# Four 512x512 weight products per group rewritten in Strassen's seven-product scheme in a cross-attention and RWKV kernel

## The chip, the cores and the metric

The kernel runs on one core of a Trainium2 chip. The metric is the device time of one execution in microseconds (us), and less is better. Arithmetic is in float32 throughout. The engines are PE (TensorE, matrix products), DVE (VectorE), ACT (ScalarE), POOL (GpSimd) and SP (SyncE, which here only issues transfers).

## The reference

There are 32 sequences of 128 tokens with 512 features. A first layer normalizes each sequence and its context, and forms an attention with a 512x512 score matrix per sequence. A second layer is an RWKV block over them:

```python
xa = _ln(x, ln1_w, ln1_b)
sx = concat([state[:, 1:2] - xa[:, :1], xa[:, :-1] - xa[:, 1:]])
xxx = tanh((xa + sx * maa_x) @ maa_w1)          # five low-rank mixes
xk, xw, xv, xr, xg = xa + sx * (maa_stack + xxx @ maa_w2)
w = exp(-exp(time_decay + tanh(xw @ td_w1) @ td_w2))
r, k, v = xr @ Wr.T, xk @ Wk.T, xv @ Wv.T
g = silu(xg @ Wg.T)                             # gates
out = recurrence over time of (r, k, v, w, u)
x1 = x + groupnorm(out) * g @ Wo.T
xc = _ln(x1, ln2_w, ln2_b)                      # feed-forward part
xk2, xr2 = xc + sx2 * ffn_maa_k, xc + sx2 * ffn_maa_r
rr = sigmoid(xr2 @ Wfr.T)
kk = square(relu(xk2 @ Wfk.T))
return x1 + rr * (kk @ Wfv.T)
```

All of `Wr, Wk, Wv, Wg, Wo, Wfk, Wfr, Wfv` are 512x512. The change concerns the products with `Wg`, `Wfk`, `Wfr` and `Wfv`.

## The kernel before, in words

The 32 sequences go through in 8 groups of four (`G = 4`), so that a group has N = 512 tokens. `layer0(b)` is the first layer for one sequence, and `layer1(g, xs)` the RWKV block for one group. In the block, activations lie with 128 features on the partitions and the 512 tokens of the group along the row: an activation is four such tiles (`NC = 4`). The sequences of the next group are worked off inside the current one (`ahead`), so that PE has independent work at any moment. The feed-forward part (`feed_forward`) of a group has three stages, `norm`, `squares` (`Wfk`) and `rows` (`Wfr`, `Wfv`). That of the last group but one is held back (`later`) and used as filler inside the last group, which has no next group.

A product with a whole weight is 16 matmuls of 128x128 against 512 columns. `proj` takes the weight's blocks as the held side and streams the tokens; its output has features on the partitions. The stages `head` and `rows` hold the token blocks and stream the weight, so that their output has tokens on the partitions, as the output array wants it. Four matmuls accumulate in one bank of PSUM, which has eight banks of 128x512 (`banks`). In the stage `gates`, ACT takes the sigmoid of each bank and DVE multiplies it with the bank. In `squares`, ACT takes relu of the bank and DVE multiplies it with the bank once more. In `rows`, ACT takes the sigmoid of the `Wfr` bank, DVE multiplies it with the `Wfv` bank, POOL adds the residual, and SP issues the transfer out.

The `mixes` stage between front and gates puts five mixed inputs into four tiles each: DVE reads a bank and one tile, POOL adds `xa`. That is 20 additions of 128x512 per group on POOL.

Weights are read from HBM into a ring of four 1 MB tiles (`weights`, `W_SLOTS`), once per group. Working tiles of 128x512 come from a pool of 44 (`work`, `T_SLOTS`), tiles of twice the width from a pool of 3 (`wides`).

Nothing is issued when it is written. `Program.record` (line 246, which is why nearly every row of the profile has that line) collects every operation, and `schedule` puts them in order with an own table of durations (`cost`), the delays between engines (`LAGS`), the slots of the pools, and shifts of each stage's rank (`SHIFTS`). The result is one fixed order per engine, in which each engine then waits for what it needs. `pace` makes some transfers wait for a PE instruction.

Of the kernel before, what the change touches and what calls it, by code (L numbers as in the profile page):

```python
# [12 lines left out]
F32 = mybir.dt.float32  # L13
# [16 lines left out]
DM, NMIX, DD = 32, 5, 64  # L30
C = 64
LEVELS = (4, 8, 16, 32)
T_SLOTS, SMALL_SLOTS, W_SLOTS, WIDE_SLOTS = 44, 40, 4, 3
# [30 lines left out]
    "first0": -306, "first0+": -95, "first1": 2, "first1+": -122, "first2": -40,  # L64
    "first2+": -7, "first3": 24, "first3+": 203, "front": 7, "front+": 157, "gates": -67,
    "gates+": -1, "head": -121, "head+": 51, "levels0": -68, "levels0+": -71, "levels2": 20,
    "levels2+": -152, "mixes": 81, "mixes+": -41, "norm": 78, "norm+": -310,
    "outputs0": -277, "outputs0+": 238, "outputs2": -235, "outputs2+": -661,
    "recurrence0": -14, "recurrence0+": -48, "recurrence2+": -68, "rows": 85, "rows+": 306,
    "squares": -88, "squares+": 77, "values0": -56, "values0+": -63, "values2": 33,  # L70
    "values2+": 81,
# [82 lines left out]
class Fixed(Pool):  # L154


    def shaped(self, slot, shape):
        return self.tiles[0]
# [450 lines left out]
def xattn_then_rwkv(ctx: ExitStack, tc: tile.TileContext, a: dict, out: bass.AP):  # L609
# [9 lines left out]
    work = Pool(slots("t", T_SLOTS, [P, 512]))  # L619
    small = Pool(slots("small", SMALL_SLOTS, [P, 64]))  # L620
    rks = Pool(slots("rk", 2, [P, 4 * N]))
    wides = Pool(slots("wide", WIDE_SLOTS, [P, 2 * N]))
    weights = Pool(slots("wring", W_SLOTS, [P, NC * E]))
# [16 lines left out]
    def st_(*shape):  # L640
        return View(Tensor(small, [P, *shape]))
# [9 lines left out]
    for n in ("WnT", "WmT", "Wl0", "WoT0"):  # L651
        w0[n] = const.tile([P, P], F32, tag=n, name=n)
        nc.scalar.dma_start(w0[n], a[n])
# [26 lines left out]
    wv = fixed("wv", [P, NC, E])  # L680

# [92 lines left out]
    def weight(n, after):  # L774
        K.held = after
        t = View(Tensor(weights, [P, NC, E]))
        K.sync.dma_start(t, a[n + "T"].rearrange("(c p) o -> p c o", p=P))
        return t
# [98 lines left out]
    def proj(w, xm, eo):  # L877

        pp = bank()
        for ci in range(NC):  # L880
            K.tensor.matmul(
                pp, w[:, ci, eo * P : (eo + 1) * P], xm[ci], start=(ci == 0), stop=(ci == NC - 1)
            )
        return pp

# [16 lines left out]
    def recurrence(c, ex, xk, xr, xv, wk, wr, s0m):  # L902
# [5 lines left out]
        for i in range(2):  # L908
            K.scalar.copy(r[i], proj(wr, xr, c + i))
            K.scalar.copy(k[i], proj(wk, xk, c + i))  # L910
            K.scalar.copy(v[i], proj(wv, xv, c + i))
# [189 lines left out]
    def layer1(g, xs):  # L1101
# [41 lines left out]
        wg, wk, wr = (weight(n, begun[g * G + 1]) for n in ("Wg", "Wk", "Wr"))  # L1143
# [77 lines left out]
        gates = []  # L1221
        for c in range(NC):
            pg = proj(wg, xm["g"], c)
            gate = wt()
            K.scalar.activation(gate, pg, AF.Sigmoid)
            K.vector.tensor_tensor(gate, pg, gate, ALU.mult)
            gates.append(gate)

        o = []
        for c in range(0, NC, 2):  # L1230
            K.stage = ("recurrence", g, str(c))
            if g == NG - 1 and c == 2:
                last_ws[:] = [weight(n, holds) for n in ("Wfk", "Wfr")]
            holds = K.ops[-1]
# [11 lines left out]
        if g == NG - 1:  # L1246
            last_ws.append(weight("Wfv", third))
        elif g < NG - 2:
            ws = [weight(n, third) for n in ("Wfk", "Wfr", "Wfv")]

# [28 lines left out]
        for i in range(G):  # L1279
            px1 = bank()  # L1280
            for c in range(NC):
                K.tensor.matmul(
                    px1, o[c][:, i * L : (i + 1) * L], wo[:, c, :],
# [7 lines left out]
        if g == NG - 2:  # L1291
            later.append(feed_forward(g, xs, last_ws))
        else:
            place(3)
            for _ in feed_forward(g, xs, ws if g < NG - 1 else last_ws):
                pass
        return following

    later, last_ws = [], []

    def feed_forward(g, xs, ws):

        K.stage = ("norm", g, "")
# [13 lines left out]
        kk = []  # L1317
        for eo in range(NC):
            pk = proj(ws[0], xk2, eo)
            t = wt()  # L1320
            K.scalar.activation(t, pk, AF.Relu)
# [71 lines left out]
```

## Time and profile before

| what | value |
|---|---|
| median of 3 runs | 1794.67 us (1794.45 to 1796.84) |
| profiled execution | 1798.06 us, of which its span is 1796.3 us |
| granted PE clock in it | 0.995 |
| PE busy | 1758.5 us, 98% of the span |
| DVE, ACT, POOL busy | 1171.4, 706.2 and 310.3 us |
| moved by DMA | 87.23 MB, mean 49 GB/s |

The span runs from the first to the last instruction of the profiled execution. A float32 matmul shows up as two PE records, each with its own load of the held side (engine PEld): 512 matmuls are x1024. In a row's names the streamed operand comes first and the held one second: `bank<-t,wring` streams an activation past weights, `bank<-wring,t` streams a weight past activations. Records of PE overlap each other in the trace, so that the mean of one record is longer than the distance from one to the next.

### The profile page before, as it was taken

The numbers are of one execution on the slowest core, as the hardware profiler recorded it, in microseconds if no ns is written. First come the engines' busy times: TensorE is split into PE (matmuls) and PEld (weight loads), VectorE is DVE, ScalarE is ACT, GpSimd is POOL, SyncE is SP. The second block draws the span as 40 slices with busy tenths as digits, with TensorE's granted clock in tenths as the row PEclk, the third lists the DMA queues.
The fourth block names the chain that finished last, engine by engine and source line by source line (L and its number), as shares of the span: only waits on it lengthen the run. The fifth ranks groups of instructions, "written<-read, shape, count | busy, mean of one in ns | idle before, by whom it ended". The sixth has DMA issues, their size and how long they took to land. (4 is left out here: it accounts for less than half of the span.)

```text
span 1796.3 us, 45435 instructions
## 1 busy us (share of the span) xinstructions
PE 1758.5 (98%) x20232; PEld 888.7 (49%) x20232; DVE 1171.4 (65%) x2301; ACT 706.2 (39%) x1230; POOL 310.3 (17%) x329
## 2 busy tenths in 40 slices
PE   8999999999999999999999999999999999899998
PEld 4435554456434554345543465445554345445543
DVE  9847784468935687456864578546784765786561
ACT  4524531356313563235632445324542245324321
POOL 2230014200150001600006000160010500320011
PEclk9999999999999999999999999999999999899999
DMA  6000131012120130101211022110221201001010
GB/s 206 21 0 3 37 119 62 9 41 73 59 70 1 41 108 26 69 2 53 96 47 47 2 58 90 53 41 2 63 85 59 73 25 49 3 0 61 15 36 35
DMA packets 61940, 87.23 MB, mean 49 GB/s; under 512 B 20336, under 2 KB 21488, under 8 KB 61744
## 3 DMA queue, kind: packets, MB, share of 16 engines
q1 hardware_dynamic: 61024, 84.06, 14.7%
q8 instruction: 158, 2.59, 0.6%
q14 instruction: 38, 0.31, 0.1%
q10 hardware_dynamic: 720, 0.26, 0.1%
HBM read 75.93 MB, written 8.39 MB: 47 GB/s over the span
## 5 line engine op out<-in xcount | busy, mean ns | idle before, releaser
L246 PE MATMUL bank<-t,wring 128*128 128x512 f32 x1024 | 469.0, 603 | 2.0 <-DVE t L246 2.0
L246 PE MATMUL bank<-wring,t 128*128 128x512 f32 x768 | 339.6, 595 | 0.7 <-DVE t L246 0.7
L246 PEld LDWEIGHTS bank<-t,wring 128*128 128x128 f32 x1024 | 187.2, 190 | 239.1 <-issue 205.4
L246 POOL TENSOR_TENSOR t<-t,t 128x512 f32<-128x512 f32 x192 | 239.4, 1285 | 349.3 <-DVE t L246 343.3
L246 DVE TENSOR_TENSOR t<-bank,t 128x512 f32<-128x512 f32 (+1 forms) x256 | 143.7, 585 | 211.4 <-PE bank L246 164.1
L246 POOL TENSOR_TENSOR small<-small,neg_half 128x1 f32<-128x1 f32 (+1 forms) x96 | 62.9, 661 | 1131.4 <-DVE small L246 1131.3
L246 PE MATMUL bank<-t,t 128*128 128x512 f32 x512 | 251.1, 607 | 2.1 <-ACT t L246 1.9
L246 PEld LDWEIGHTS bank<-wring,t 128*128 128x128 f32 x768 | 143.5, 190 | 185.7 <-issue 179.1
L246 ACT COPY t<-bank 128x512 f32<-128x512 f32 (+1 forms) x240 | 132.2, 589 | 218.3 <-PE bank L246 212.1
L246 ACT ACTIVATE t<-bank 128x512 f32<-128x512 f32 x120 | 71.4, 598 | 341.4 <-PE bank L246 341.3
L246 DVE SCALAR_TENSOR_TENSOR t<-bank,vec,t 128x512 f32<-128x512 f32 x192 | 131.4, 743 | 67.2 <-PE bank L246 67.2
L246 PEld LDWEIGHTS bank<-ident,t 128*128 128x128 f32 x900 | 104.5, 141 | 75.2 <-issue 43.6
L246 PE MATMUL bank<-ident,t 128*128 128x128 f32 x900 | 130.1, 276 | 4.6 <-ACT t L246 2.7
L246 ACT ACTIVATE wide<-rk,par 128x512 f32<-128x512 f32 x128 | 85.4, 715 | 122.4 <-DVE rk L246 122.4
L246 ACT ACTIVATE t<-bank,small 128x512 f32<-128x512 f32 x128 | 87.8, 690 | 106.2 <-DVE small L246 105.4
L246 PEld LDWEIGHTS bank<-t,t 128*128 128x128 f32 x512 | 87.0, 189 | 85.6 <-issue 56.3
L246 PEld LDWEIGHTS bank<-wide,rk 32*64 32x64 f32 x8192 | 95.6, 131 | 55.3 <-ACT wide L246 17.0
L246 PE MATMUL bank<-t,wv 128*128 128x512 f32 x256 | 122.6, 603 | 0.0
L246 DVE COPY_PREDICATED at<-level,bank 128x512 f32<-128x512 int32 x192 | 121.5, 704 | 0.0
L246 PE MATMUL bank<-wide,rk 32*64 32x64 f32 x8192 | 105.9, 233 | 8.2 <-issue 3.8
L246 DVE TENSOR_REDUCE small<-bank 128x1 f32<-128x512 f32 x128 | 85.9, 680 | 30.8 <-PE bank L246 30.4
L246 DVE SCALAR_TENSOR_TENSOR t<-t,vec,t 128x512 f32<-128x512 f32 x128 | 90.9, 755 | 0.1
(98 smaller groups left out, 1796.4 us busy)
## 6 DMA issues: line engine op xcount, KB each, us to landing
t<-in_ctx_dram SPq DMA_DIRECT2D x32, 256.0 KB, 3.2
t<-in_x_dram SPq DMA_DIRECT2D x32, 256.0 KB, 3.0
wring<-in_WgT_dram SPq DMA_DIRECT2D x8, 1024.0 KB, 5.2
wring<-in_WkT_dram SPq DMA_DIRECT2D x8, 1024.0 KB, 5.3
wring<-in_WrT_dram SPq DMA_DIRECT2D x8, 1024.0 KB, 5.2
wring<-in_WoT_dram SPq DMA_DIRECT2D x8, 1024.0 KB, 5.6
out_dram<-t SPq DMA_DIRECT2D x32, 256.0 KB, 2.0
wring<-in_WfkT_dram SPq DMA_DIRECT2D x7, 1024.0 KB, 5.2
```

Source lines behind the costliest of these rows:

```text
L246: done[op] = f(*[real(x) for x in args], **{k: real(x) for k, x in kw.items()})
```

## The change

The four products are computed with seven products of half the size in each direction instead of eight, in the form with 15 additions (Winograd's form of Strassen's scheme). Both sides are cut into four quarters of 256x256. One product of quarters is four matmuls of 128x128 against 256 columns, so that a weight takes 28 matmuls of 256 columns, where it took 16 of 512.

The seven combinations of the weight's quarters are computed once, in the first group, by four additions on POOL, and the ones that are no quarter are saved in HBM (`saved`). Later groups read all seven, 256 KB each (`seven`). The combinations of the activations (`s1`, `s2`, `s4` and one in place) are formed on POOL, as eight additions of 128x256 per product. The sums of the products are formed partly in PSUM, by going on accumulating in a bank after ACT has copied it out (`p1`, `p5`, `u2`, `u3`), partly by DVE from a bank and a copy, and one of them on POOL.

The other stages follow from that. The gates are now multiplied on POOL from tiles, after a sigmoid of a tile. The squares are two ACT passes over double-width tiles. The rows come out as four tiles of two sequences and half the features: DVE multiplies, POOL adds the residual in two halves, and SP writes 256 KB. The ring of weights becomes 16 tiles of 256 KB, `Wk`, `Wr` and `Wo` being read in four pieces, and the wide pool has 6 tiles. The transfers of the feed-forward weights are ordered after the operation `after` in front of its `norm` stage; before, they were ordered after one in the recurrence (`third`). The planner's shifts are other numbers.

```diff
+H = 256
+LEFT, RIGHT = ("Wg", "Wfk"), ("Wfr", "Wfv")
-T_SLOTS, SMALL_SLOTS, W_SLOTS, WIDE_SLOTS = 44, 40, 4, 3
+T_SLOTS, TINY_SLOTS, SMALL_SLOTS, W_SLOTS, WIDE_SLOTS = 43, 36, 6, 16, 6
...
-    weights = Pool(slots("wring", W_SLOTS, [P, NC * E]))
+    weights = Pool(slots("wring", W_SLOTS, [P, 2 * H]))
...
+    def seven(n, g, after):
...
+        left = n in LEFT
+        if g:
+            return [
+                piece(saved[n, i] if (n, i) in saved else quarter(*QUARTERS[left][i]))
+                for i in range(7)
+            ]
+        q11, q12, q21, q22 = (piece(quarter(i, j)) for i in range(2) for j in range(2))
+        s1, s2, s4 = (View(Tensor(weights, [P, 2, H])) for _ in range(3))
+        if left:
+            K.gpsimd.tensor_tensor(s1, q12, q22, ALU.add)
+            K.gpsimd.tensor_tensor(s2, s1, q11, ALU.subtract)
+            K.gpsimd.tensor_tensor(s4, q21, s2, ALU.subtract)
+            K.gpsimd.tensor_tensor(q12, q11, q12, ALU.subtract)
+            got = [q11, q21, s1, s2, s4, q12, q22]
...
+    def winograd(w, x, to, left=True):
+        def part(i, j):
+            return [x[2 * i + k][:, j * H : (j + 1) * H] for k in range(2)]
+        s1, s2, s4 = (wt([P, 2, H]) for _ in range(3))
...
+        if left:
+            steps = [(s1, x12, x11, ALU.subtract), (s2, x22, s1, ALU.subtract)]
+            steps += [(x12, x22, x12, ALU.subtract), (s4, x21, s2, ALU.subtract)]
+            sides = [x11, x21, s1, s2, x22, x12, s4]
...
+        for to_, one, other, op in steps:
+            for k in range(2):
+                K.gpsimd.tensor_tensor(to_[k], one[k], other[k], op)
+        def product(i, into, first):
+            with K.bunch(1720):
+                for m in range(2):
+                    for k in range(2):
+                        of_m = slice(m * P, (m + 1) * P)
+                        one, other = (
+                            (w[i][:, k, of_m], sides[i][k]) if left
+                            else (sides[i][k][:, of_m], w[i][:, k])
+                        )
+                        K.tensor.matmul(
+                            into[:, m], one, other, start=first and m == 0 and k == 0,
+                            stop=k == 1, skip_group_check=True,
+                        )
...
+        pb = new_bank()
+        product(0, pb, True)
+        p1 = copy(pb)
+        pa = new_bank()
+        product(1, pa, True)
+        K.vector.tensor_tensor(to(0, 0), pa, p1, ALU.add)
+        pc = new_bank()
+        product(2, pc, True)
+        p5 = copy(pc)
+        product(3, pb, False)
+        u2 = copy(pb)
+        product(4, pc, False)
+        K.vector.tensor_tensor(to(0, 1), pc, u2, ALU.add)
+        product(5, pb, False)
+        u3 = copy(pb)
+        K.gpsimd.tensor_tensor(to(1, 1), u3, p5, ALU.add)
+        pd = new_bank()
+        product(6, pd, True)
+        K.vector.tensor_tensor(to(1, 0), pd, u3, ALU.add)
...
-            pg = proj(wg, xm["g"], c)
-            gate = wt()
-            K.scalar.activation(gate, pg, AF.Sigmoid)
-            K.vector.tensor_tensor(gate, pg, gate, ALU.mult)
+        winograd(
+            seven("Wg", g, begun[g * G + 3]), xm["g"],
+            lambda i, j: gates[i].view(j * H, (N, 2), (1, H)),
+        )
+        for gate in gates:
+            t = wt()
+            K.scalar.activation(t, gate, AF.Sigmoid)
+            K.gpsimd.tensor_tensor(gate, gate, t, ALU.mult)
...
-            pk = proj(ws[0], xk2, eo)
-            t = wt()
-            K.scalar.activation(t, pk, AF.Relu)
-            K.vector.tensor_tensor(t, t, pk, ALU.mult)
+        winograd(seven("Wfk", g, after), xk2, lambda i, j: kk[i].view(j * H, (N, 2), (1, H)))
+        for t in kk:
+            for func in (AF.Relu, AF.Square):
+                K.scalar.activation(t, t, func)
...
+        winograd(seven("Wfr", g, after), xr2, lambda i, j: rr[i][j], left=False)
+        for t in rr[0] + rr[1]:
+            K.scalar.activation(t, t, AF.Sigmoid)
+        winograd(seven("Wfv", g, after), kk, lambda i, j: y[i][j], left=False)
+        for i in range(2):
+            for j in range(2):
+                t, first = y[i][j], g * G + 2 * i
+                K.vector.tensor_tensor(t, t, rr[i][j], ALU.mult)
+                for m in range(2):
+                    K.gpsimd.tensor_tensor(
+                        t[:, m], t[:, m], xs[2 * i + m][:, j * H : (j + 1) * H], ALU.add
+                    )
```

## The prediction

> **What bounds the kernel now.** I read the page's first section, then the list of PE's own waits, then the windows of one group, and only then single rows.
>
> ```profile
> PE 1758.5 (98%) x20232; PEld 888.7 (49%) x20232; DVE 1171.4 (65%) x2301; ACT 706.2 (39%) x1230; POOL 310.3 (17%) x329
> ...
> PE bank L246 <- issue: 8.2, 11, 1.4
> PE bank L246 <- DVE t L246: 8.2, 7, 2.0
> PE bank L661 <- DMA WoT<-in_WoT_dram: 6.1, 1, 6.1
> PE bank L246 <- ACT t L246: 4.7, 10, 1.8
> ```
>
> PE is busy for 98% of the span, and its waits add up to some 30 us, of which 6.1 are the first transfer. The chain that ended last says little here: for its last 180 us it is PE alone. So the order that the planner made keeps PE filled, and the time is PE's streaming time. What PE no longer streams is gained, unless something else becomes late.
>
> ```profile
> 725.00:762.00 37.00, 36.95 (x117) 14.09 (x117) 17.55 (x26) 8.46 (x11) 29.66 (x24) 1.00 0.16 57
> ...
> 1538.00:1640.00 102.00, 94.08 (x1329) 46.02 (x1330) 81.51 (x135) 34.70 (x53) 27.94 (x25) 0.95 0.01 2
> ```
>
> The columns after the window are length, PE, PEld, DVE, ACT, POOL, clock, DMA share, GB/s. The first window is one group's mixes: POOL is busy for 29.66 of 37 us, although its mean is 17%. The second is the last group's front, mixes and first recurrence, where less filler is left: there PE loses 8 us, and DVE is at 80%. Those are the two tight places.
>
> **PE's part: what is removed and added.**
>
> ```profile
> 499.64 10.89 PE L246 MATMUL bank<-wring,t 128*128 128x512 f32 x25
> 899.68 6.17 PE L246 MATMUL bank<-wring,t 128*128 128x512 f32 x14
> 1293.25 1.73 PE L246 MATMUL bank<-wol,t 128*128 128x128 f32 x14
> 862.61 0.39 PE L246 MATMUL bank<-wol,t 128*128 128x128 f32 x2
> ```
>
> From start and length of uninterrupted runs: 512 columns take (10.89 - 6.17) / 11 = 0.429 us per record, 128 columns (1.73 - 0.39) / 12 = 0.112 us. No 256-column float32 record exists. Between the two rows a straight line gives 0.2175; half of 512 gives 0.2145. I take 0.2165.
> Removed: 4 products x 8 groups x 16 matmuls x 2 records = 1024 x 0.429 = 439.4 us. Added: 4 x 8 x 28 x 2 = 1792 x 0.2165 = 388.0 us. Saved: 51 us (49.6 with 0.2175, 55 with 0.2145).
>
> A rule of the Trainium skill speaks against this step. "TensorE: Matmul & The Clock Gate", sections "LDWEIGHTS" and "Back-to-back issue gap": a load takes about columns / 1.2 ns, so 107 ns for 128, and the spacing of load and matmul pairs is set by both. In series 0.2165 would become 0.32 us, the added part 578 us and the kernel 139 us slower. The row decides: the 128-column run has a new held side for each record, and still has 0.112 us per record. So a load shorter than the stream behind it is hidden there, and 256 columns leave twice the cover. PEld rows of this kind have 190 ns, still under 216.
>
> **The other engines, per group.**
> - POOL gains 32 additions of 128x256, 4 sums `u3 + p5`, 4 gate multiplications; the residual additions only change shape. Whole ones have 1285 ns. A half has no row: it lies between 0.6 (a one-column operation, 597 ns) and 1.27, and I take 0.68, a little over half. That is 32 x 0.68 + 8 x 1.27 = 32 us, 256 us in all, and 16 x 1.27 = 20 us for the weights of the first group. POOL goes from 310 to about 585 us, 33%.
> - DVE loses 12 multiplications with a bank and gains 12 sums from a bank and 4 multiplications of tiles (0.69 each): +2.8 us, 22 us in all, 68%.
> - ACT gains 16 copies (589 ns) and 1.8 us in the squares (4 passes of 1057 ns for 4 of 598): +11 us, 90 us in all, 45%.
> - DMA: each product reads 1.75 MB where it read 1 MB, about 24 MB more on 87; the engines' share goes from some 15% to 19%. Next group's `Wk` and `Wr` hold 8 of the 16 ring slots during a feed-forward, so that its 21 pieces turn over in the other 8: one slot every 14 us, while a 256 KB transfer lands in 3.0 to 3.2 us. SP issues some 460 transfers in place of 175; behind one that waits for its slot stand the next pieces, `Wo` and the outputs, with some 10 us to spare each. I cost this at nothing; if the cover were gone, each late piece would cost PE up to 3 us.
> None of these sums binds, each lying beside PE. What counts is what is late locally.
>
> **What POOL and DVE do to each other.**
>
> ```profile
> L246 DVE SCALAR_TENSOR_TENSOR t<-bank,vec,t 128x512 f32<-128x512 f32 x192 | 131.4, 743 | 67.2 <-PE bank L246 67.2
> L246 DVE TENSOR_TENSOR t<-rk 128x512 f32<-128x512 f32 x48 | 31.7, 686 | 5.2 <-PE bank L246 4.3
> L246 DVE TENSOR_TENSOR t<-wide 128x512 f32<-128x512 f32 x16 | 15.5, 971 | 55.4 <-ACT wide L246 55.4
> ...
> 757.66 3.75 POOL L246 TENSOR_TENSOR t<-t,t 128x512 f32<-128x512 f32 x3
> 760.37 1.59 DVE L246 TENSOR_TENSOR t<-wide 128x512 f32<-128x512 f32 x1 [5.79 <-ACT wide L246]
> ```
>
> The second and third rows are the same work, both operands from SBUF, and yet 686 and 971 ns. The `t<-wide` one sometimes comes when POOL is still at the mixes: the one at 760.37 takes 1.59 us and ends 0.55 us after POOL's last, so it waited for POOL. The mixes' own operation, with one operand from PSUM, runs beside POOL throughout at 743. "SBUF — State Buffer", section "SBUF: two separate sides", has the rule: a DVE operation with two SBUF inputs and a GpSimd one take one port pair in turn, and the loser is blocked for the other's whole instruction. That speaks against putting the additions on POOL.
> By the rule: in one feed-forward POOL has 24 x 0.68 + 3 x 1.27 + 8 x 0.68 = 25.6 us, and DVE about 25 operations of the blocked kinds (12 mixes at 0.75, 3 shifts, 4 multiplications at 0.69, some scalings), 17 us. In turn 43 us, beside 3 x 28 x 2 x 0.2165 = 36.4 us of PE plus some 3.4 us of the next group's scores. Read strictly, 3 us are lost per group. By the trace, a hit costs about 0.9 us (1.59 - 0.69), and what it does to PE depends on who is next. So I go through it. In the new order the eight additions for `Wfk` stand beside eight DVE mixes of `xk2`, `xr2` and the next front. In turn they take 8 x (0.68 + 0.75) = 11.4 us, not 5.4. Then s1 comes 1.4 us late and s2 by 0.5 us; DVE comes some 5.5 us late to the sum that frees the bank which the seventh `Wfk` product reuses, and PE waits about 1.9 us for it. After that PE has 12 us of `Wfr` products, which cover relu, square and the additions for `Wfv`. So 0 to 2.4 us are lost per group, and I take 1.7: 14 us in all. The mixes give little: their DVE operations read PSUM, and PE has some 36 us of work beside POOL's 31 from the first mix to the last gate product. The gate multiplications fall on the start of the recurrence: 4 us in all. The first group has 15 us more on POOL in its feed-forward (12 weight additions): 4 us. The last group and the tail (one more DVE step of 0.7 us between the last product and the transfer): 2 us.
>
> **Sum.** 1796.3 - 51 + 24 = 1769 of span, -27 us. The profiled run had 1798.06 us, 3.4 above the median of the runs, so I apply the difference to the median: 1794.7 - 27 = 1767.7, rounded to 1767.
>
> **The rivals.**
> A, the forecast (0.50): 8 to 38 of the 51 us come back as short PE waits, most in the feed-forward stages. 1752 to 1782.
> B (0.32): nearly all is kept, because PE's fillers cover the lateness, as they do now in the crowded mixes window (36.95 of 37 us). At most 8 us come back, and up to 55 are saved: 1740 to 1752. For it: the waits of before are only 30 us in 1796. Against it: those fillers were as long, and the additions on POOL were not there.
> C, the slower side (0.18, of which 0.08 slower): the port in turn. Its place is the stretch from the first `Wfk` addition to the last gate product, where POOL now has some 63 us (25.6, then 20 mixes at 1.27 and 12 for the gates) beside about 92 of PE (48.5 for the four products, the rest scores, mixes and the first projections of the recurrence). It decides from 51 / 8 = 6.4 us per group; at 8 us per group the time is 1795 + 13 = 1808. For it: the strict sum of 43 us against 40. Against it: DVE's sums read a bank, and that kind was never slowed.
> That the change doesn't do what it says can be left aside: the new order has 896 matmuls of 256 columns and 512 fewer of 512.
>
> The measurement of this kernel can tell about 0.2% (3.6 us). Faster by more: A, B and a third of C, 0.88. Within: 0.04. Slower: 0.08. The range leaves out the upper half of C and a sliver of B: 1742 to 1789.
>
> **What would show it.** Right: PE rows of 128x256 whose runs have 0.215 to 0.218 us per record; PE busy near 1710 us; POOL near 585; PE's waits grown to 50 or 60 us, most of them on POOL and DVE tiles around the `Wfk` products; the DVE rows with two tile operands with a longer mean than 755 ns. Wrong: a 256-column pitch over 0.23; PE waits on DMA of `wring`; PE's waits as small as before (B), or over 80 us (C).

## The result, and the profile after

The changed kernel takes 1820.77 us (median of three runs, 1813.12 to 1821.34) against 1794.67: a ratio of 1.0129, 95% interval 1.0086 to 1.0171. It is some 26 us slower; the prediction had it 27 us faster.

The page of the changed kernel, busy time by engine. The helper that records every operation, L246 before, is L252 here.

```profile
PE 1730.7 (95%) x21000; PEld 1039.4 (57%) x21000; DVE 1275.9 (70%) x2333; ACT 797.2 (44%) x1363; POOL 643.6 (35%) x697
```

PE's own waits (us in total, times, longest):

```profile
PE bank L252 <- POOL t L252: 23.9, 11, 5.7
PE bank L252 <- ACT t L252: 16.2, 16, 4.7
PE bank L252 <- DVE t L252: 13.8, 22, 1.3
PE bank L252 <- issue: 10.1, 13, 2.7
PE bank L672 <- DMA t<-in_WoT_dram: 6.1, 1, 6.1
PE bank L252 <- DMA wring<-Wfv: 4.1, 4, 1.2
```

These and four small ones add up to 78 us where they were 32, and they come from four sides at once. No engine is full: POOL, whose new additions will turn out to be the largest part of the cause, is idle for 65% of the span. The 11 waits on POOL are only 24 of the 78 us.

Two windows, one around a steady group's feed-forward additions and one at the last group (columns: length, PE, PEld, DVE, ACT, POOL, granted clock, DMA share, GB/s). The first row is the kernel before, at the same time of its run; the other two are the changed kernel. The last window has the bounds of the one that the prediction called tight.

```profile
695.00:711.00 16.00, 16.00 (x50) 7.03 (x49) 13.67 (x28) 5.27 (x9) 0.54 (x1) 1.00 0.01 2
695.00:711.00 16.00, 12.49 (x58) 10.37 (x57) 15.97 (x23) 5.29 (x9) 13.55 (x14) 1.00 0.32 93
1538.00:1640.00 102.00, 96.18 (x985) 49.95 (x983) 63.43 (x113) 32.30 (x52) 39.33 (x39) 0.95 0.03 9
```

In the last window PE is busy for 96.18 us where it was 94.08, so this stretch did not get worse. In the steady group DVE is busy for 15.97 of 16 us and POOL for 13.55, while PE has 3.5 us without work. This is how a shared resource looks in a table by engine: both sharers seem busy, because an instruction that waits inside itself counts as busy. The single rows show it. From the trace of the changed kernel, start, length, engine, operation, count, and in brackets the idle time before the first of them and what ended it:

```profile
694.84 8.80 PE L252 MATMUL bank<-t,wring 128*128 128x256 f32 x40
694.28 6.88 DVE L252 SCALAR_TENSOR_TENSOR t<-t,vec,t 128x512 f32<-128x512 f32 x6
694.90 10.91 POOL L252 TENSOR_TENSOR t<-t,t 128x256 f32<-128x256 f32 x10
705.93 1.97 PE L252 MATMUL bank<-t,wring 128*128 128x256 f32 x8 [2.30 <-POOL t L252]
706.51 1.28 ACT L252 ACT_TABLE_LOAD   x1 [7.37 <-DVE tiny L252]
708.49 0.58 ACT L252 COPY t<-bank 128x512 f32<-128x512 f32 x1
709.12 1.99 PE L252 MATMUL bank<-t,wring 128*128 128x256 f32 x8 [1.22 <-ACT t L252]
```

Six mixes on DVE take 6.88 us, 1.15 each, and ten additions on POOL 10.91, 1.09 each. Undisturbed a mix follows the last one after 0.67 us, and an addition the last one after 0.68 (nine of them from 261.08 on, in the first group). Here the two alternate: the mixes start at 694.28, 695.41, 696.54 and so on, one mix and one addition every 1.13 us. So the s-operand (a combination of quarters that a product streams) of `Wfk` comes 2.30 us late. What follows isn't POOL's any more: DVE reaches its reductions late; ACT has waited 7.37 us for one of them, and behind that instruction in ACT's queue stands the copy that PE needs next, 1.22 us more. The same two waits come, within a few hundredths of a us, in three of the four groups that follow the first, with a third of 0.85 us at the first `Wfr` products; the remaining group has 2.29 and 0.64.

Where the time is lost along the kernel is read from the first `heads` product of each group (start times in the trace):

| us | 1st mark | to 2nd | to 3rd | to 4th | to 5th | to 6th | to 7th | to 8th | to the end |
|---|---|---|---|---|---|---|---|---|---|
| before | 224.0 | 219.3 | 218.3 | 218.7 | 219.1 | 220.3 | 246.4 | 145.9 | 84.3 |
| after | 216.1 | 223.0 | 218.9 | 222.6 | 220.1 | 219.0 | 251.2 | 162.4 | 85.7 |

PE's stream is 6.4 us shorter per group, but a steady group is as long as before; from the sixth mark on (for short, the last groups) the kernel is 22.7 us longer (4.8 + 16.5 + 1.4), which is the whole difference of the two profiled runs (1819.0 - 1796.3). The 224.0 at the start is on the long side: the two runs with pauses below, whose first group is the same as before's, have 219.1 and 220.3. So the first six groups are some 4 us slower rather than equal.

One quantity is in none of these rows: the mean granted clock is 0.984 where it was 0.995. With the clock records the span splits into three parts that add up: PE's work (busy time less what half clock adds to it), PE's idle time with all gaps counted, and what half clock adds while PE is busy. The two rows of runs without the additions are explained in the next section.

| us | PE's work | idle | added by half clock | span |
|---|---|---|---|---|
| before | 1750.9 | 37.8 | 7.5 | 1796.3 |
| after | 1707.6 | 88.3 | 23.1 | 1819.0 |
| additions left out | 1704.7 | 59.7 | 11.4 | 1775.8 |
| memsets for additions | 1704.3 | 51.2 | 14.8 | 1770.3 |

The change takes 43 us off PE's work, and adds some 50 us of idle time and 16 us of half clock.

### The profile page after: what moved, and what is told of

It reads as the page before. It is cut to its first block, busy times and chain, and to the rows that moved or that the text cites. A ratio compares the mean times of both kernels' runs of the same rounds, so it can differ in the third digit from the quotient of the medians.

```text
span 1819.0 us, 48427 instructions
## 1 busy us (share of the span) xinstructions
PE 1730.7 (95%) x21000; PEld 1039.4 (57%) x21000; DVE 1275.9 (70%) x2333; ACT 797.2 (44%) x1363; POOL 643.6 (35%) x697
## 4 chain that ended last, share of the span: by engine, by line
PE 74%; DVE 15%; ACT 4%; issue 2%; DMA 2%; POOL 1%; SPq 1%; POOLq 0%; DVEq 0%; ACTq 0%
PE bank L252 74%; DVE t L252 10%; DVE tiny L252 3%; ACT t L252 2%; DMA t<-in_ctx_dram 1%; ACT at L252 1%; POOL t L252 1%; ACT wide L252 1%; DVE rk L252 1%; DMA wring<-Wfv 1%; SPq L252 1%; DVE wide L252 0%; DVE at L252 0%; POOL wide L252 0%; DVE at L635 0%
## 5 line engine op out<-in xcount | busy, mean ns | idle before, releaser
L252 PE MATMUL bank<-t,wring 128*128 128x256 f32 (+1 forms) x1408 | 455.0, 472 | 28.7 <-POOL t L252 23.9
L252 POOL TENSOR_TENSOR t<-t,t 128x256 f32<-128x256 f32 (+1 forms) x384 | 399.0, 1070 | 130.9 <-DVE t L252 83.4
L252 ACT COPY t<-bank 128x512 f32<-128x512 f32 (+1 forms) x368 | 207.4, 587 | 430.8 <-PE bank L252 403.9
L252 PEld LDWEIGHTS bank<-t,wring 128*128 128x128 f32 x1408 | 263.9, 194 | 180.5 <-issue 93.7
L252 POOL TENSOR_TENSOR tiny<-tiny,neg_half 128x1 f32<-128x1 f32 (+1 forms) x96 | 62.8, 661 | 852.5 <-DVE tiny L252 852.5
L252 PE MATMUL bank<-wring,t 128*128 128x256 f32 (+1 forms) x896 | 255.9, 442 | 9.2 <-ACT t L252 4.2
L252 PE MATMUL bank<-t,t 128*128 128x512 f32 x512 | 255.8, 607 | 2.6 <-ACT t L252 1.5
L252 DVE TENSOR_TENSOR t<-bank,t 128x512 f32<-128x512 f32 (+1 forms) x240 | 132.0, 580 | 150.0 <-PE bank L252 139.3
L252 PEld LDWEIGHTS bank<-wring,t 128*128 128x128 f32 x896 | 169.6, 191 | 91.8 <-issue 62.1
L252 DVE SCALAR_TENSOR_TENSOR t<-bank,vec,t 128x512 f32<-128x512 f32 x192 | 131.3, 744 | 46.7 <-PE bank L252 46.6
L252 PEld LDWEIGHTS bank<-ident,t 128*128 128x128 f32 x900 | 105.7, 142 | 98.7 <-issue 48.9
L252 PE MATMUL bank<-ident,t 128*128 128x128 f32 x900 | 137.4, 279 | 14.5 <-DVE t L252 9.5
L252 ACT ACTIVATE wide<-rk,par 128x512 f32<-128x512 f32 x128 | 85.6, 717 | 116.1 <-DVE rk L252 107.4
L252 PEld LDWEIGHTS bank<-t,t 128*128 128x128 f32 x512 | 85.5, 191 | 79.1 <-issue 53.8
L252 ACT ACTIVATE t<-bank,tiny 128x512 f32<-128x512 f32 x128 | 88.0, 690 | 93.7 <-DVE tiny L252 70.5
L252 PE MATMUL bank<-t,wv 128*128 128x512 f32 x256 | 124.1, 594 | 0.0
L252 PEld LDWEIGHTS bank<-wide,rk 32*64 32x64 f32 x8192 | 94.3, 130 | 51.8 <-ACT wide L252 13.7
L252 DVE COPY_PREDICATED at<-level,bank 128x512 f32<-128x512 int32 x192 | 120.4, 706 | 0.0
L252 PE MATMUL bank<-wide,rk 32*64 32x64 f32 x8192 | 104.3, 232 | 8.1 <-issue 5.4
L252 DVE TENSOR_REDUCE tiny<-bank 128x1 f32<-128x512 f32 x128 | 86.3, 684 | 17.4 <-PE bank L252 16.3
L252 DVE TENSOR_SCALAR t<-t,tiny,tiny 128x512 f32<-128x512 f32 x128 | 72.9, 582 | 31.3 <-POOL tiny L252 30.9
L252 ACT ACTIVATE t<-bank,vec 128x512 f32<-128x512 f32 x64 | 45.0, 790 | 112.1 <-PE bank L252 112.0
```

The lines of the kernel that those rows point to most:

```text
L252: done[op] = f(*[real(x) for x in args], **{k: real(x) for k, x in kw.items()})
```

## The experiments

Two theories to begin with. *Port*: POOL's additions and DVE's operations with both operands in SBUF are served in turn, and the lateness travels to PE through queues. *Order*: the new plan simply has less slack, whatever POOL reads. Later ones: POOL's queue is just too long (*length*); PE's pauses cost more than their length through the clock (*clock*); the last groups; and the quality of the planner's search.

### The additions left out, or moved to DVE, in the same order

Both take the list of instructions as planned and change it only where it is issued.

```diff
+            if op.tag == "s" and op.stage[1] > 0:     # adds_out
+                continue
...
+                if op.tag == "s":                       # adds_dve
+                    attr = "vector"
                 f = getattr(getattr(self.nc, attr), method)
```

Left out:

> The changed kernel with the same order of work and the same slots; only the 32 additions of activation halves per group (s1, s2, s4 and the one in place) are left out from the second group on: the products then stream whatever is in their tiles, which leaves these sums out of the computation. Nothing is replanned. Port theory (POOL's additions and DVE's operations with two SBUF operands take one port in turn, and the lateness travels down DVE's and ACT's queues to PE): the waits before Wfk and Wfr go, DVE's mixes of the feed-forward have 0.74 us again in place of 1.21, PE's idle time falls from 74 to 35 or 45 us, half-clock periods become fewer, and the time falls to 1765 to 1785. Order theory (the new plan has less slack, whatever POOL does): the waits stay in the last two groups, time 1805 to 1820.

Measured: 1780.43 us, ratio to before 0.992 (0.9895 to 0.9944), 40 us under the changed kernel. The mixes have their old mean again:

```profile
L255 DVE SCALAR_TENSOR_TENSOR t<-t,vec,t 128x512 f32<-128x512 f32 x96 | 67.2, 750 | 0.0
```

PE's waits fell from 78 to 50 us, a little less far than expected. So 40 of the 77 us that went missing (51 of stream, and 26 of longer time) hang on the additions, and order alone is not the cause. Whether it is their reading or their length stays open here. The first group kept its additions and its longest wait (5.75 us).

On DVE:

> The changed kernel with the same order and slots; the 32 additions of activation halves per group are issued on DVE at the same places in place of POOL (some 0.42 us each there, 108 us in all, DVE to about 75%). Port theory: no taking in turn between the additions and the mixes, since one engine does both: 8 additions and 8 mixes of the feed-forward take 8 x (0.42 + 0.745) = 9.3 us in place of 11.4 for the pair, so the wait of 2.3 us at Wfk shrinks by about 1.5, but beside the mixes of the next gates DVE's additions can now meet POOL's 128x512 ones. Time 1795 to 1815. Order theory: no change, 1815 to 1825. If DVE's own length counts most: slower, over 1825.

Measured: 1833.62 us, ratio 1.021 (1.0181 to 1.024): 13 us slower than the changed kernel, the third case of the expectation. The waits on POOL are down to 3.6 us, but the same copies on ACT are later (1.56 and 2.19 us in every steady group, `bank<-t,wring <- ACT t` and `bank<-wring,t <- ACT t`): DVE's own queue is now the longer one. So there is no room for the additions on DVE at those places either, though DVE is busy for only 74% of this run's span.

### Additions that nobody waits for, in the kernel before

```diff
+            for one, other in op.pads:                  # after xk2, xr2, kk, xm["g"]
+                self.nc.gpsimd.tensor_tensor(self.pad, real(one), real(other), ALU.add)
```

> The kernel before with its own order and slots, and 32 additions of 128x256 on POOL per group that nobody waits for: eight after the mixes of xk2, eight after those of xr2, eight after the squares, eight after the gate mixes, written to one tile of its own. They cost POOL about 0.7 us each (180 us in all) and nothing on PE. Port theory: DVE operations with two SBUF operands that meet them take 1.2 us in place of 0.74, POOL's own next sums come late, and PE loses 10 to 30 us: 1805 to 1825. Order theory: POOL at 28% has room, nothing waits for these sums, so within 4 us of the kernel before.

Measured: 1822.82 us, ratio 1.0151 (1.0119 to 1.0184), which is what the port theory said. But the trace says that it was right for another reason (start, length, operation, count, idle before; then the mixes' group with count, total and mean ns):

```profile
484.75 14.17 POOL L248 TENSOR_TENSOR pad<-t,t 128x256 f32<-128x256 f32 x16 [14.08 <-DVE t L246]
498.88 0.54 POOL L246 TENSOR_TENSOR small<-small,neg_half 128x1 f32<-128x1 f32 x1
499.46 0.55 DVE L246 TENSOR_SCALAR t<-t,small,small 128x512 f32<-128x512 f32 x1 [12.19 <-POOL small L246]
500.66 2.56 PE L246 MATMUL bank<-wring,t 128*128 128x512 f32 x4 [1.87 <-DVE t L246]
```

```profile
L246 DVE SCALAR_TENSOR_TENSOR t<-t,vec,t 128x512 f32<-128x512 f32 x128 | 91.7, 760 | 0.1
```

The additions came after the mixes, not beside them, and the mixes kept 760 ns. What cost time was POOL's queue: a one-column power of 0.54 us, which DVE needs for the next normalization, stood behind sixteen additions, DVE waited 12.19 us for it, and DVE's products for the squares stood behind that. In the last group PE waited 11.93 us at once for a POOL operation behind such a row. So this run is no evidence for the port. It shows that a long row on POOL can cost as much by itself, and that an expectation can be met for the wrong reason.

### The same time on POOL without its reads

This is the run that tells port and length apart. Each addition becomes two memsets of the same half, with the same producers waited for and the same products waiting.

```diff
+            if op.tag == "s":
+                x = self.nc.gpsimd.memset(real(op.calls[0][2][0]), 0.5)
+                for b in op.fed:
+                    self.tc.add_manual_dep(x.ins, done[b].ins.name, ...)
+                done[op] = self.nc.gpsimd.memset(real(op.calls[0][2][0]), 0.5)
+                continue
```

> The changed kernel with its own order and slots; each of the 32 additions of activation halves per group is replaced on POOL by two memsets of that half (about 0.7 us for the two, the time of one addition), which wait for the same mixes and for which the products wait as before. These sums are so left out of the computation; POOL's occupation and the order of waits stay, and only the reading of SBUF by POOL is gone. Port theory (it is the shared port): DVE's mixes have 0.74 us again and the time is near that without the additions, 1780 to 1792. Length theory (POOL is simply too slow for its place in the order): the wait of 2.3 us before the Wfk products stays, 1810 to 1822. If a memset takes the port as well: DVE's rows stay at 1.2 us and the time at 1815 to 1825.

Measured: 1773.52 us, ratio to before 0.9888 (0.9867 to 0.991), so 47 us under the changed kernel. DVE has 39 us less with the same instructions. POOL has 575 us against 644: two memsets are busy for 0.63 us, an undisturbed addition for 0.73, which makes 26 us of the difference, and the rest is what POOL's operations waited for the port. First the page:

```profile
PE 1719.1 (97%) x21000; PEld 1035.9 (59%) x21000; DVE 1236.9 (70%) x2333; ACT 796.4 (45%) x1363; POOL 574.8 (32%) x953
```

Half of the memsets, and DVE's mixes (groups: count, total, mean ns):

```profile
L261 POOL MEMSET t<- 128x256 f32 x240 | 75.2, 313 | 13.7
L265 DVE SCALAR_TENSOR_TENSOR t<-t,vec,t 128x512 f32<-128x512 f32 x96 | 67.3, 755 | 0.0
```

One stretch of DVE and PE (start, length):

```profile
677.10 5.38 DVE L265 SCALAR_TENSOR_TENSOR t<-t,vec,t 128x512 f32<-128x512 f32 x8
679.46 10.74 PE L265 MATMUL bank<-t,wring 128*128 128x256 f32 x49
```

The mixes' group of the changed kernel, and of the kernel before, is

```profile
L252 DVE SCALAR_TENSOR_TENSOR t<-t,vec,t 128x512 f32<-128x512 f32 x96 | 92.7, 1018 | 0.0
L246 DVE SCALAR_TENSOR_TENSOR t<-t,vec,t 128x512 f32<-128x512 f32 x128 | 90.9, 755 | 0.1
```

Eight mixes take 5.38 us where six took 6.88, with POOL working all the while, and PE runs 49 of the 56 `Wfk` records without a pause. In the steady groups the length theory is out: a POOL that is nearly as long in its place, but does not read SBUF, brings no wait at `Wfk`. In the feed-forward of the last group it holds: there PE still waits 4.08 us for the memsets, against 4.45 for the additions and 1.54 with nothing in their place. Some 47 us go with the reads; the memsets being a tenth of a us shorter than an addition, this is rather an upper bound.

What is left is not all explained. The marks of this run are 213.3, then 215.2, 214.1, 216.6, 213.0, 213.0, 244.8, 154.8, 85.5. Up to the sixth mark it is 34.5 us shorter than the kernel before, but from there on it is 485.1 us long, 8.5 more than before, where PE's work is 8.2 us less: 17 us are lost there, 8 as idle time and 9 by half clock. With the additions left out the same stretch is 477.4 us long, and 10 are lost. So, by one profiled run each, 7 of the 17 go with POOL's time in its place, and 10 stay with nothing there.

The port is not wholly gone from this run either, since POOL still reads SBUF for the gate multiplications and the sums of products. DVE operations that overlap one of POOL's and are over 25% longer than the fastest tenth of their kind are longer by 91 us together in the changed kernel, by 51 here and by 18 before. But nearly all of the increase lies up to the sixth mark, where little is lost; from there on it is 12 us against 10 before. So these meetings are unlikely to be what costs the 17 us.

### PE's pauses by themselves

Memsets on POOL wait for PE's last product, and PE's next product for them; eight in one place per group, or one in each of four.

```diff
+                if op.stage[1] in range(1, 6) and (op.stage[0], n) in PAUSES:
+                    ... # 8 memsets at one place, or 1 at each of four
```

> The kernel before, with one artificial pause of PE in each of five groups (the second to the sixth): between two products of the squares eight memsets of 128x512 on POOL wait for PE's last product and PE's next product waits for them, some 3 to 5 us. Clock theory: every such pause is followed by a period of 3.4 to 6.8 us at half clock, which costs half its length again, so five pauses cost 5 x (pause + 2 to 3.4 us). Rival: the clock doesn't fall for so short a pause, and the cost is 5 x the pause alone.

Measured: 1823.55 us in one run. PE's waits on them are 23.8 us, 4.76 each:

```profile
PE bank L264 <- POOL pad L252: 23.8, 5, 4.8
```

From the second to the sixth `heads` mark the kernel is 902.4 us long, against 876.4 before, which is 6.5 us per pause over the four groups: 1.7 us more than the pause, a little under the clock theory's 2 to 3.4, and far from the rival's nothing. Two windows (the clock is the third column from the end) show where they are:

```profile
483.00:490.70 7.70, 3.00 (x7) 0.98 (x6) 2.27 (x6) 0.60 (x1) 4.74 (x9) 0.83 0.00 0
490.70:494.00 3.30, 3.28 (x4) 1.51 (x5) 0.54 (x1) 0.60 (x1) 0.00 (x0) 0.50 0.00 0
```

PE returns at 490.7 and works its first 3.3 us at a clock of 0.50. Every one of the five pauses has a half-clock period of 3.4 or 6.8 us with it; in two of them part of it lies inside the pause. What half clock adds while PE works is 1.9 us per pause in the four groups, enough for the 1.7.

> The kernel before, with four artificial pauses of PE in each of five groups (two in the squares, two in the rows), each one memset of 128x512 on POOL between two products: by the long pauses (eight memsets, 4.76 us) one memset gives 4.76 - 7 x 0.58 = 0.7 us, 14 us in all. Clock theory: so short a pause brings no half-clock period, and the group gets longer by 4 x 0.7 = 2.8 us, no more (the long ones: 6.7 us for 4.76), 1805 to 1812. Rival: every pause costs more than its length: 1815 to 1825.

Measured: 1816.69 us in one run, above the clock theory's range and in the rival's. Here the twenty pauses, of 0.65 to 1.2 us, bring no half-clock period; but they cost more than is recorded. The waits, and a window with two of them:

```profile
PE bank L264 <- POOL pad L252: 16.3, 20, 1.2
```

```profile
484.00:495.00 11.00, 9.65 (x23) 4.09 (x23) 4.06 (x9) 1.79 (x3) 1.60 (x3) 1.00 0.00 0
```

16.3 / 20 = 0.8 us each by the waits, but the marks give (895.9 - 876.4) / 4 groups / 4 pauses = 1.2 us. So both are partly right: a short pause keeps the clock and costs about 0.4 us beyond its record, a long one costs 1.7 us more, with the clock. Why the 0.4 us are not in the rows isn't settled: ends of matmuls are modelled in the trace, and the first records after a pause are spaced wider, 1.97 us for eight of 256 columns in the row of 705.93 above, against 0.38 + 7 x 0.216 = 1.89 in an undisturbed row.

### Which products, and which groups

Replanned each, so that the order's own effect is in them. In one, the predicate is `n != "Wg"`, in the other `g < NG - 2`; products outside it are as in the kernel before. A new plan alone moves the changed kernel by 20 us, as the searches further down show, so that neither of these two runs decides anything by itself.

```diff
+    def parts_of(n, g):
+        return n != "Wg"            # only_ff;   g < NG - 2 for not_last
```

> The changed kernel replanned, with the scheme only in the three products of the feed-forward; the gates take plain products as before. The order is a new one, so its own effect of some 10 us either way is in it. Port theory (the additions of the feed-forward meet DVE's mixes, those of the gates give little): about as slow as the changed kernel or slower, 1815 to 1835, since 13 us of PE's saving are gone and the waits before Wfk stay. If the gates' additions at the crowded mixes cost as much as the others: 1795 to 1812.

Measured: 1822.8 us, ratio 1.0156 (1.0139 to 1.0173), in the port theory's range: with a quarter of the saving gone the time is the same as with all four. PE waits 26.3 us for POOL.

> The changed kernel replanned, with the scheme in the first six groups and the four products of the last two groups as in the kernel before. Theory of the last groups (they have the least other work beside them and lost all of the 23 us): the last two groups get back to the length they had, 22 us less than the changed kernel, 1796 to 1802; the first six break even. Port theory alone: the loss of the last groups goes, but a new order brings losses of its own: 1790 to 1812. If the last groups' loss were not from the additions: 1815 or more.

Measured: 1803.67 us, ratio 1.0048 (1.0032 to 1.0063), 17 us under the changed kernel, in the port theory's range and just above that of the last groups. From the sixth mark on it has 483.6 us in place of 499.3, not the 476.6 of before. Up to there it is as long as the changed kernel (1318.0 and 1319.7 us).

### A planner that knows the port

The planner gets one more resource: POOL's tensor operations, and DVE's without an operand in PSUM, exclude each other. For each such kernel the stages' shifts were searched anew with the planner's own estimate of the end as the measure; two more runs make a search without the port. That search was about a third as long, so the comparison isn't quite even.

```diff
+def uses_port(engine, method, outs, ins):
+    if engine == "POOL":
+        return method == "tensor_tensor" and size(outs[0]) > 8
+    if engine != "DVE" or method not in ("tensor_tensor", "scalar_tensor_tensor", "tensor_scalar"):
+        return False
+    return size(outs[0]) > 1 and not any(v.tensor.pool.tiles[0].name.startswith("bank") for v in ins)
...
+                if op.port:
+                    start = max(start, port)
```

> The changed kernel with one thing more in the planner: POOL's tensor operations and DVE's operations without an operand in PSUM share a port, and one starts in the plan only when the other has ended. The stages' shifts were searched anew for this planner. Its own estimate of the end is 1719 us, against 1716 for the changed kernel without the port and 1749 for the kernel before. Port theory: since the order now allows for the taking in turn, fewer of PE's waits come as a surprise; most of the 47 us that the memsets gave back stay lost where the port is truly full (the feed-forward), but part comes back: 1775 to 1800. If the port is full whatever the order: 1800 to 1815.

> Control: the kernel before with the planner that knows the port, and shifts searched as long; the planner's estimate goes from 1749 to 1746. It tells what the new planner and the search give by themselves. Port theory: the order of before has few such meetings, so within 5 us of the kernel before, 1789 to 1799. If the search alone makes the difference: under 1787.

> The changed kernel with its own planner, which does not know the port, and only the stages' shifts searched anew; the planner's own estimate of the end goes from 1716 to 1704 us. Port theory: the estimate is blind to what costs the time, so the gain does not arrive, 1810 to 1830. Search theory (any fresh search gives 15 to 20 us): 1795 to 1805.

> The kernel before with its own planner and only the shifts searched anew (estimate 1749.5 to 1748.1). Port theory: the port-aware planner gave this kernel 15 us because its order keeps the few meetings apart; without it the gain is small, 1787 to 1797. Search theory: 1777 to 1785.

> The port-aware order of the changed kernel, with the 32 additions per group replaced by two memsets of the same half each (these sums are left out of the computation). If the port-aware order still loses to the port: it falls from 1800 to 1770 to 1780. If that order has taken the taking in turn into account and what is left are waits that it planned: within 8 us of 1800.

| kernel | us | ratio to before (95%) | planner's estimate |
|---|---|---|---|
| after, own planner, new search | 1799.98 | 1.0023 (1.0013 to 1.0032) | 1704 |
| after, planner with the port | 1800.47 | 1.0025 (1.0012 to 1.0037) | 1719 |
| the same order, memsets for additions | 1775.18 | 0.9882 (0.9855 to 0.991) | - |
| before, own planner, new search | 1797.55 | 1.0016 (1.0006 to 1.0026) | 1748 |
| before, planner with the port | 1779.63 | 0.9916 (0.9901 to 0.9931) | 1746 |

The port theory of the planner missed for both kernels. For the changed kernel a new search gives 20 us without knowing the port, as the search theory had it and against the port theory's 1810 to 1830; knowing the port gives nothing on top (1800.47 is at the edge of the two ranges, 1775 to 1800 and 1800 to 1815). For the kernel before the search gives nothing (it is 3 us slower), which was the port theory's side; but the port-aware search gives 15 us, where that theory had allowed 5. By its own expectation that run spoke for the search alone; the search without the port then took this away. Part of why can be read from DVE's rows: the DVE operations that overlap one on POOL and are over 25% longer than the median of their kind are longer by 17.6 us together before, by 17.4 with the search alone and by 8.3 with the port-aware plan. A few meetings can be kept apart by an order. The changed kernel, with 256 additions more, has many left: measured against the fastest tenth of a kind, as above, 90 us after the search alone and 75 with the port-aware plan. Its mixes and PE's largest wait in the port-aware order:

```profile
L245 DVE SCALAR_TENSOR_TENSOR t<-t,vec,t 128x512 f32<-128x512 f32 x96 | 81.7, 899 | 4.7 <-PE bank L245 4.1 <-POOL t L245 0.6
```

```profile
PE bank L245 <- DVE t L245: 29.0, 19, 5.6
```

In the port-aware order the mixes still have 899 ns, and PE waits 29 us for DVE in place of POOL. Memsets in the same order still give back 25 us, as the first side of its expectation had it. So no order of this planner that was tried makes the reads free. How much of the 15 us of the kernel before is the port, and how much a lucky search (the last groups gained most, 468.2 against 476.6 us; its start has 216.4, where the same first group took 219.1 to 224.0 in three runs), isn't separated by one pair of runs.

### The gates alone, and the first six groups, with that planner

> The scheme for the gates' product alone (13 us of PE's stream saved), with the planner that knows the port and shifts searched for it; the planner's own estimate is 1736 against 1749 for the kernel before. Port theory: the gates' additions stand beside DVE's mixes that read PSUM and take no port, so most of the 13 us is kept: 1778 to 1790. Rival (POOL is 80% busy at the mixes, and its sums come late there): 1792 to 1802.

Measured: 1781.85 us, ratio 0.992 (0.9905 to 0.9935), inside the port theory's range. But its reason doesn't hold beside the control: the kernel before with the same planner has 1779.63. So the gates' 13 us of stream have not been kept either; from the second to the fifth mark its groups are 218.2, 218.4 and 218.2 us long and those of the control 218.3, 218.0 and 218.1. From start to start of PE's records, waits left out, those of 512 and 256 columns take 173.5 us of such a group in place of 175.3; the smaller ones take 1.0 more, and PE is idle for 0.8 more. Whether the port or the longer way to the gates does that is open.

> As the kernel with the scheme in the first six groups, with the planner that knows the port; its own estimate is 1728. If both causes add up (17 us for the last groups, and what the port-aware order gives): 1770 to 1792. If the plan's surprises in the first six groups stay: 1795 to 1805.

Measured: 1799.44 us, ratio 1.003 (1.0017 to 1.0042), the second side of the expectation. The causes don't add up. The steady groups have 220 to 224 us here, with a wait of some 5 us for DVE in each of the first ones, as in the port-aware order above.

The fastest kernel that computes everything is then the one without the scheme and with the port in its planner (1779.63 us); the gates' version is as fast, and both beat the two kernels of the comparison.

## Why the prediction was wrong, step by step

The balance, from the medians: -51 (stream) + 47 (reads of the additions, by the memsets) + 30 (the rest) = +26. The prediction had 24 for the 47 and the 30 together. The split belongs to this one order: in the port-aware order it is -51 + 25 + 32 = +6.

The step that failed is the price of the additions: the prediction followed the wait for one operand and let PE's `Wfr` products cover the rest, 1.7 us per group, where the runs show 5.9. Next to it, the last groups, sized 2 us, lose 17 even with memsets, and the clock, left out, adds 16, part of it in those groups. The steps one by one:

- *The stream: right.* 256-column records follow each other after (10.74 - 8.80) / (49 - 40) = 0.216 us, from the uninterrupted row of 49 above and one of 40 in the changed kernel. The prediction took 0.2165, and loads are hidden, as it had decided from the row. Adding load and stream in series was its own reading: the Trainium skill, "TensorE: Matmul & The Clock Gate", section "Back-to-back issue gap", calls the two pipelined. PE's busy time is 1731 and not 1710, of which half clock makes 16; its work is 43 us less and not 51, and the 8 are open (ends of matmuls are modelled).
- *The bounds of the engines: roughly right, and no use.* POOL 644 us (585 predicted), DVE 70% (68), ACT 44% (45), DMA 21% on the main queue (19 predicted). None binds.
- *The port at `Wfk`: the size of the first wait nearly right, but by luck; its effect wrong.* "0 to 2.4 us are lost per group, and I take 1.7": PE waits 2.30 us on POOL there. The prediction had the first two sums (`s1`, `s2`) late and then a bank that DVE frees; but PE ran five of the seven products without a pause (40 records from 694.84), and waited for an operand from POOL before the sixth in its order and for a copy by ACT before the seventh. The next sentence of the prediction fails outright, that PE then "has 12 us of `Wfr` products, which cover" the rest. The prediction followed one operand; it did not follow DVE's queue, which is some 5 us late after the row of mixes, and from there ACT's queue, whose copy is needed 3 us later (1.22 us), and a further copy at the first `Wfr` products (0.85 us). The rule of the Trainium skill ("SBUF — State Buffer", section "SBUF: two separate sides": the loser is blocked for the whole instruction of the other) agrees in that they take turns, but not in the size: a pair takes 1.13 us, less than 0.67 + 0.68 one after the other, and less than the 1.43 of the prediction. The strict sum, 43 us of port against 40 of PE, makes it 3 us per group, while the reads cost 47 / 8 = 5.9. So the loss is not that the port is full; it is lateness at particular instructions.
- *"DVE's sums read a bank, and that kind was never slowed": true and beside the point.* They are not slowed, they queue behind operations that are.
- *The first group: sized 4 for the weights' sums; the wait was another.* One half addition for the activations took 5.75 us, and PE waited for all of it:

```profile
252.62 5.38 DVE L252 SCALAR_TENSOR_TENSOR t<-t,vec,t 128x512 f32<-128x512 f32 x8
253.44 5.75 POOL L252 TENSOR_TENSOR t<-t 128x256 f32<-128x256 f32 x1 [0.76 <-DVE t L252]
259.25 7.00 PE L252 MATMUL bank<-t,wring 128*128 128x256 f32 x20 [5.75 <-POOL t L252]
```

- *The last group and the tail: sized 2, measured 17 with memsets and more with the reads.* The feed-forward of the second last group is the filler of the last group's recurrence, so its additions meet the recurrence's operations there:

```profile
1677.47 11.01 POOL L252 TENSOR_TENSOR t<-t,t 128x256 f32<-128x256 f32 x10
1676.85 5.75 DVE L252 SCALAR_TENSOR_TENSOR t<-t,vec,t 128x512 f32<-128x512 f32 x5
1687.55 1.15 ACT L252 ACTIVATE t<-t 128x512 f32<-128x512 f32 x2 [8.76 <-DVE t L252]
1689.23 1.12 PE L252 MATMUL bank<-ident,t 128*128 128x128 f32 x4 [4.72 <-ACT t L252]
```

The prediction had named the last group's front and first recurrence (1538 to 1640) as tight, but priced the change there by its one added step; that stretch stayed as it was, and the loss came behind it. Of the 17 us, POOL's time makes 7; that the other 10 are the order's is argued and not shown: they remain with the additions left out, and what in the order does it was not separated.
- *The clock: left out.* Its page had it, 0.95 in the last group's window. Half clock adds 16 us more than before (23.1 against 7.5); 8 of them go with the reads (14.8 with memsets), so they are in the 47, and 7 in the 30.
- *DMA at nothing: nearly right.* Pieces of `Wfv` come late in four groups, 4.1 us in all.

Rival C had the mechanism and the place, at a chance of 0.08 for slower. Its price was too high for what it priced (8 us per group, where the reads cost 5.9), and its 1808 us are near the measured time by terms that it did not have. By its break-even of 6.4 us per group the reads alone would have left the kernel a little faster; the last groups and the rest of the clock put it on the other side. What spoke against it was an argument about one kind of operation, where the question was about a queue.

## What to carry to other kernels

Before moving work to an idle engine, list which instructions of other engines will stand beside it, and whether they share a port; then follow the lateness through every in-order queue behind them until an instruction that PE needs. A sum of busy times can't show it, since waiting inside an instruction counts as busy. In a kernel that is 98% PE, a pause of PE costs more than its length: here 6.5 us for one of 4.76. And compare a changed plan with the old kernel replanned as well: here that control was worth 15 us, while the best replanned version of the whole change is still 5 us slower than the kernel before.

## What the runs showed of the hardware that was not expected

- The taking in turn isn't always one for one. Beside back-to-back mixes of 0.67 us, one POOL addition was held for 5.75 us while DVE's operations ran on unhindered (253.44 above), and the next one for 1.97 us; in the later groups (694.90 above) the two alternate every 1.13 us. What decides between the two is open.
- Not only operations with two SBUF operands are slowed: of 20 `TENSOR_SCALAR t<-t,tiny` with one 128x512 operand that overlapped an addition, 18 were longer, by 0.6 us in the mean (11.4 us together). Of 155 `t<-bank,vec,t` none was.
- A POOL memset takes no turn: with 512 of them in place of the additions the mixes stay at 755 ns.
- A PE pause of 4.76 us brought a half-clock period of 3.4 or 6.8 us each time, five times in all; one of 0.65 to 1.2 us never in twenty.
